# A ring of image rows in column-mod-4 order, read by patches with a stride of three

## The chip, the cores and the metric

The kernel runs on one core of one Trainium2 chip. The metric is the device time of one execution in microseconds (us); the median of several executions counts. A profile of one further execution is there for reading: it records every instruction of TensorE (PE, with its weight loads PEld), VectorE (DVE), ScalarE (ACT), GpSimd (POOL) and SyncE (SP), and the DMA traffic.

## The reference

Two blocks follow each other on `x` (4 images, 96 channels, 128×128, fp32). The first is a state-space block with four scans; the change does not touch it. The second is an attention over convolution maps:

```
xr, x1, x2 = relu_split_norm(gn(x))
key = unfold(conv3x3(x1, aw1))     # patches of 3x3, not overlapping: 42 x 42 of them
qry = unfold(conv3x3(x2, aw2))     # 96 channels x 9 taps x 1764 patches
attn = softmax(einsum("bckl,bqkl->bqck", key, qry) / sqrt(96 * 9))
value = conv3x3(x1, aw3)
y1 = layer_norm(conv3x3(value, attn as 3x3 weights))
y2 = layer_norm(conv3x3(x2, w_conv2)) * x1
out = x + xr + conv1x1(concat(y1, y2), w_full) + b_full
```

For every tap k of the 3×3 patch, key and query are thus multiplied over all patches: 96×96 products that sum over the pixels with row ≡ kh and column ≡ kw modulo 3. An image is 128 pixels wide, and 42 patches take 126 of them: columns 126 and 127, and rows 126 and 127, are in no patch.

## The kernel before

The program works through the four images. The first block of all images comes first. Image 0 then makes its maps (key, query, value, and `c2`, the convolution with `w_conv2`) in another way (`direct_maps`, with the class `Taps`), while the first block still runs. Images 1, 2 and 3 go through `attention`: a part that makes the maps, then a short part that turns the products into weights (`weights`: softmax, transposes), then a part that applies them to the value (`own` as the output tile). The norm and split of the next image and the output of the previous one run beside it ("light" work); generators are run in turn by `co_run`, which emits the instructions of the two in a ratio of costs. The last 20 or so microseconds of each map part, where the weights are made, are a chain with little beside it.

Convolutions in `attention` run in a column-tiled form (F(4,3), Winograd's): a row of 128 pixels is 32 tiles of four columns. Six planes per map are multiplied on TensorE and summed in PSUM pairs (`two`, three buffers of two banks). `outputs` takes them out: ScalarE copies two of the three pairs to SBUF (`ends`, `odd`, L1522), VectorE builds sums and differences (L1536–L1542), and four instructions at L1544, one for each column j of the tile, write the result:

```
for k, j, f in ((1, 1, AA), (2, 0, AA * AA), (0, 0, 1.0), (3, 1, AA**3)):
    if k == 0:
        nc.vector.tensor_add(v, ends, v)
    for p, e, o in parts:
        nc.vector.scalar_tensor_tensor(
            at(o, k), rows(w[p:e, j]), f, rows(v[p:e, j]), ALU.mult, ALU.add
        )
```

`at(o, k)` says where column k of all tiles lies in the output. Outputs that are kept in column-mod-4 order (first all 32 pixels with column ≡ 0 mod 4, then those ≡ 1, and so on: `own` and `oc` of images 1 to 3) get 32 adjacent words per row; outputs in plain order get every fourth word.

The maps are made in strips of 12 rows (eleven strips, the last of 8). For each strip and for m = 0 (inputs `x1p`: key and value) and m = 1 (`x2p`: query and `c2`), a first product of 128 output channels gives 96 channels of key or query and 32 of value or `c2`; a second gives the other 64. The first one's result goes to the ring: `rings[m]` of class `PairTaps`, room for two strips of 12 rows, plain order, rows of 129 words of which the last is zero. Rows lie in the order of their residue mod 3. `first_out` then copies the 32 value or `c2` channels (partitions 96 to 127) from the ring to `own` in column-mod-4 order, with three POOL copies, one for each residue of the row (L1967), and takes the statistics of the `c2` ones on VectorE (L1962).

`both` turns a pair of ring rows: for every tap it transposes 85 columns of the flat ring, three words apart, on TensorE (L1727). With two rows of 129 words, 43 columns come from the first row and 42 from the second. At this stride a row of 129 has 43 columns instead of 42, so the last one of the first row is in no patch; ScalarE multiplies it with zero while copying the PSUM pair to `kt`, with a scale for each partition (`patches`, L1732). `multiplied` (L1617) multiplies key and query patches, 85 rows to contract, and VectorE adds the result to `sm` (L1628, L1630).

The transposes of a strip are put in a list when both maps of that strip are written (`complete`), and are taken from the list between the products of the next strip (`some`). The order of the instructions on an engine is in these parts not the order of the code, but one made by the planner of the framework when the program is built.

`c2_weights` reads the statistics of `c2` (`c2a`) and sums them up.

Of the kernel before, what the change touches and what calls it, by code (L numbers as in the profile page):

```python
# [9 lines left out]
F32 = mybir.dt.float32  # L10
# [7 lines left out]
C = 96  # L18
# [11 lines left out]
PW = W + 1  # L30
# [2 lines left out]
TN = W // TW  # L33
PB = TN + 1
PP = PB * TW
AA = 2.0
AR = 12
LR = 8
# [31 lines left out]
def kernel(  # L70
# [1434 lines left out]
    def outputs(pool, m, n, parts, later, then):  # L1505

        got = []  # L1510

        def at(v, k):
            if len(v.shape) == 4:
                return v[:, :, k]
            return v.rearrange("p h (t k) -> p h t k", k=TW)[:, :, :, k]

        def rows(v):
            return v.rearrange("p (h t) -> p h t", t=TN)

        def copy_of(x, name, bufs):  # L1520
            t = pool.tile([128, 2, AR * TN], F32, name=name, bufs=bufs)[:m, :, :n]
            nc.scalar.copy(t, x[:m, :, :n])  # L1522
            return t

        def outer(c):
            later(lambda: got.append(copy_of(c, "ends", 2)))

        def sums(a, b):
            def first():
                t = copy_of(a, "odd", 1)  # L1530
                later(lambda: combined(t))

            def combined(t):
                w = pool.tile([128, 2, AR * TN], F32, name="wide", bufs=1)[:m, :, :n]
                ends, v = got[0], b[:m, :, :n]
                nc.vector.tensor_sub(w[:, 1], t[:, 1], v[:, 1])  # L1536
                nc.vector.tensor_add(w[:, 0], t[:, 1], v[:, 1])
                nc.vector.tensor_sub(v[:, 1], t[:, 0], v[:, 0])  # L1538
                nc.vector.tensor_add(v[:, 0], t[:, 0], v[:, 0])  # L1539
# [7 lines that stand above are left out]
                later(then)  # L1547

            later(first)

        return outer, sums
# [141 lines left out]
    class PairTaps(Taps):  # L1693
# [3 lines left out]
        def __init__(self, ps, later, pool):  # L1697
            self.ps, self.later, self.pool = ps, later, pool
            self.taps = [(0, 5), (5, KK)]
            self.sm = pool.tile([C, KK, C], F32, name="sm")  # L1700
            self.rings = [
                pool.tile([128, 2, AR, PW], F32, name=f"ring{i}", tag=f"ring{i}") for i in range(2)
            ]
            for t in self.rings:
                nc.gpsimd.memset(t[:, :, :, W:PW], 0.0)
            self.todo, self.rest = [], ()

        def flat(self, m):
            return self.rings[m].rearrange("p s r w -> p (s r w)")

        def part(self, m, n):
            return pairs_of(self.ps)[:m, 0, :n]

        def both(self, s, g, ks, kept):


            k0, k1 = ks
            n = (k1 - k0) * C
            pk = pairs_of(self.ps)[: 2 * NV + 1, :, :n]
            t = self.pool.tile([2 * NV + 1, 2, 5 * C], F32, name="kt", tag="kt", bufs=2)  # L1720
            slots = min(AR, H - s * AR + 1) // 3
            for m in (0, 1):
                kept[m] = t[:, m].rearrange("p (t o) -> p t o", o=C)
                for k in range(k0, k1):
                    kh, kw = divmod(k, 3)
                    o = (s % 2 * AR + kh * slots + 2 * g) * PW + kw
                    nc.tensor.transpose(  # L1727
                        pk[:, m, (k - k0) * C : (k - k0 + 1) * C],
                        self.flat(m)[0:C, o : o + 6 * NV + 1 : 3],
                        ident,  # L1730
                    )
            self.later(lambda: nc.scalar.activation(  # L1732
                t[:, :, :n], pk, AF.Copy, scale=patches[0 : 2 * NV + 1]
            ))
            self.later.tick()
            yield 0.3 * (k1 - k0)

# [180 lines left out]
    def attention(img, at):  # L1918
# [8 lines left out]
        if not img.mapped:  # L1927
# [21 lines left out]
            for s, (r0, r) in enumerate(chunks):  # L1949
                hr = r // 2  # L1950
                for m in (0, 1):
                    t, fill, load = at.strip()
                    r3 = (r + 2) // 3 * 3
                    to = taps.rings[m][:, s % 2, :r3]

                    def first_out(m=m, r0=r0, r=r, r3=r3, to=to):
                        v = to[96:128, :, 0:W].rearrange("p (q i) (t j) -> p q i j t", q=3, j=TW)
                        if m:
                            x = to[96:128, :, 0:W]
                            for q in range(0, r, 4):  # L1960
                                k = min(4, r - q)
                                nc.vector.bn_stats(img.c2a[96:128, 3 * (r0 // AR) + q // 4], x[:, q : q + k])  # L1962
                            d = last.rearrange("p (h j t) -> p h j t", j=TW, t=TN)
                        else:
                            d = vv[96:128]
                        for q in range(3):
                            nc.gpsimd.tensor_copy(d[:, q:r3:3], v[:, q])  # L1967
                        if m:
                            nc.sync.dma_start(
                                img.c2d[64:96, r0 * W : (r0 + r) * W], last[:, : r * W]  # L1970
                            )

                    evac = outputs(
                        p2, 128, r3 * TN, [(0, 128, to[:, :, 0:W])], later, first_out
                    )
                    yield from products(
                        ps, [(0, 128, 0, t, 0, r3)], pairs[m], later, evac, True,
                        [
                            both(fill[0], load[0]), fill[1], None, load[1]
                        ],  # L1980
                    )
                    yield from taps.some(1 if m else 2)
                    jobs = [(64 * q, 64 * q + 64, 128, t, q * hr, hr) for q in range(2)]
                    if m:
                        oc = pm.tile([128, AR // 2 * W], F32, name="oc", bufs=1)
                        to = [(0, 128, oc[:, : hr * W].rearrange("p (h j t) -> p h j t", j=TW, t=TN))]

                        def then(oc=oc, s=s, r0=r0, hr=hr):
                            per = 3 if hr % 4 else 4
                            for i in range(hr // per):  # L1990
                                nc.vector.bn_stats(
                                    img.c2b[:, 2 * s + i], oc[:, i * per * W : (i + 1) * per * W]
                                )
                            for q in range(2):
                                at = (r0 + q * hr) * W
                                nc.sync.dma_start(
                                    img.c2d[0:64, at : at + hr * W],
                                    oc[64 * q : 64 * q + 64, : hr * W],
                                )
                    else:  # L2000
                        to = [
                            (64 * q, 64 * q + 64, vv[0:64, q * hr : (q + 1) * hr])
                            for q in range(2)
                        ]
                        then = value_out(r0, r)
                    evac = outputs(p2, 128, hr * TN, to, later, then)
                    rest = products(ps, jobs, pairs[m], later, evac, fill=[
                        None, None, both(fill[2], load[2]), *fill[3:]
                    ])
                    if m and r0 + r == H:  # L2010
                        taps.rest = rest
                    else:
                        yield from rest
                        yield from taps.some(1 if m else 2)
                taps.complete(s, min(r, 3 * NV - r0))
# [133 lines left out]
    def c2_weights(img, ps, pool):  # L2149
# [2 lines left out]
        n = NSTRIP  # L2152
        mva, mvb = (pool.tile([128, 2], F32, name=f"mv_{i}") for i in "ab")
        for mv, st, p, e, k in (
            (mva, img.c2a, 96, 128, 4 * n - 1 if img.mapped else 3 * n - 1),
            (mvb, img.c2b, 0, 64, 2 * n - (not img.mapped)),
            (mvb, img.c2b, 64, 128, 2 * n - 1),
        ):
            v = st[p:e, :k].rearrange("p c s -> p (c s)")
            nc.vector.bn_aggr(mv[p:e], v)  # L2160
# [461 lines left out]
```

## Time and profile before

| what | value |
|---|---|
| median of 3 runs | 6576.74 us (6551.26 to 6590.82) |
| the profiled execution | 6563.7 us, of it span 6561.8 us |
| PE busy | 5379.6 us (82%) |
| DVE busy | 4887.7 us (74%) |
| ACT busy | 3826.6 us (58%) |
| POOL busy | 3510.5 us (53%) |
| mean granted clock of TensorE | 0.883 |
| maps of image 1, 2, 3 (span of L1727's stretches) | 3832–4530, 4718–5518, 5740–6332 us |

Busy times are unions over an engine's own instructions, so they say nothing alone on which engine sets the time. A row of the groups gives line, engine, operation, tiles, shape and count, then busy time and mean duration in nanoseconds, then the idle time of the engine right before them and what ended it. "two" is a PSUM pair, "ring", "kt", "own", "oc", "sm" are the tiles named above; "L1544" is a line of the kernel.

### The profile page before, as it was taken

To read this page: it belongs to the slowest core of one execution; us is meant where nothing else is said; L and a number is where in the kernel's file an instruction comes from. 1 tells how busy PE (TensorE), PEld (TensorE's weight loads), DVE (VectorE), ACT (ScalarE), POOL (GpSimd) and SP (SyncE) were. 2 spreads that over 40 slices of the span, in tenths; PEclk is the share of its full clock that TensorE was granted. 3 is DMA by queue.
4 is the path that set the end of the run, shared out by engine and by line. 5 is a ranking of instruction groups with operands and counts; after the bars stand their busy time and mean duration, and the time that the engine had idled before them with its cause. 6 is when DMAs were issued, how large, how long until landed. Compare 5 with 4: busy or idle time off the path is not lost. (4 is left out here: it accounts for less than half of the span.)

```text
span 6561.8 us, 75955 instructions
## 1 busy us (share of the span) xinstructions
PE 5379.6 (82%) x23264; PEld 2347.1 (36%) x23264; DVE 4887.7 (74%) x7229; ACT 3826.6 (58%) x4800; POOL 3510.5 (53%) x2649
## 2 busy tenths in 40 slices
PE   6889988987887735999897688877879777888888
PEld 2333323322222112444333243444324444344553
DVE  3247778988998778889745885587765788887866
ACT  1247767777787676777534554565444664544542
POOL 2236758978888546979521454465134574043420
PEclk9999989998998667999998788987988887998899
DMA  7767777775766757665676766655776555865658
GB/s 165 173 156 187 194 207 193 218 206 158 222 182 170 216 161 229 200 202 173 197 194 182 211 168 172 161 148 156 204 191 164 141 158 153 226 169 150 179 150 216
DMA packets 865058, 1198.50 MB, mean 183 GB/s; under 512 B 215598, under 2 KB 716054, under 8 KB 852172
## 3 DMA queue, kind: packets, MB, share of 16 engines
q1 hardware_dynamic: 841036, 1138.70, 63.7%
q0 software_dynamic: 16208, 38.42, 2.2%
q10 hardware_dynamic: 7408, 16.53, 0.8%
q8 instruction: 187, 3.06, 0.2%
q14 instruction: 219, 1.79, 0.1%
HBM read 777.82 MB, written 345.62 MB: 171 GB/s over the span
## 5 line engine op out<-in xcount | busy, mean ns | idle before, releaser
L622 PE MATMUL bank<-y,wp 128*128 128x512 f32 (+3 forms) x3584 | 1314.4, 624 | 85.9 <-DMA y<-y 34.6
L855 POOL TENSOR_TENSOR y<-y,dl 128x1024 f32<-128x1024 f32 x384 | 1059.3, 2759 | 267.8 <-DVE dl L847 245.7
L822 POOL TENSOR_TENSOR dl<-dl,u 128x1024 f32<-128x1024 f32 x384 | 1010.1, 2630 | 253.7 <-ACT dA L798 122.7
L843 DVE TENSOR_TENSOR_SCAN dA<-dA,pBC 128x512 f32<-128x512 f32 x768 | 981.5, 1278 | 30.7
L1451 PE MATMUL two<-ya,wd 128*64 128x192 f32 (+3 forms) x2376 | 597.2, 430 | 212.1 <-ACT odd L1522 102.4
L736 PE MATMUL pBC<-xr,wbc 60*128 60x512 bf16 (+1 forms) x1536 | 461.7, 405 | 326.3 <-DVE dA L843 253.5
L622 PEld LDWEIGHTS bank<-y,wp 128*128 128x128 f32 (+3 forms) x3584 | 457.3, 169 | 752.5 <-issue 655.0
L847 DVE TENSOR_TENSOR dl<-dA,pBC 128x512 f32<-128x512 f32 x768 | 528.0, 688 | 264.0 <-PE pBC L736 191.2
L2094 PE MATMUL bank<-y,wn 128*64 128x384 f32 (+5 forms) x2408 | 673.0, 504 | 54.5 <-DMA y<-x1d 31.6
L1897 ACT COPY yb<-ya 64x768 f32<-64x768 f32 (+1 forms) x660 | 537.9, 815 | 209.8 <-PE two L1451 138.8
L665 ACT ACTIVATE dl<-pd,dtb 128x512 f32<-128x512 f32 x768 | 485.6, 684 | 191.0 <-PE pd L736 167.3
L1451 PE MATMUL two<-yb,wd 128*64 128x192 f32 (+3 forms) x2376 | 569.8, 412 | 1.9 <-ACT yb L1897 1.9
L826 DVE TENSOR_TENSOR pBC<-dl,pBC 128x512 f32<-128x512 f32 x768 | 527.6, 687 | 8.3 <-POOL dl L822 7.3
L2094 PEld LDWEIGHTS bank<-y,wn 128*64 128x64 f32 (+3 forms) x2408 | 308.2, 168 | 345.9 <-issue 166.8
L798 ACT ACTIVATE dA<-dl,negA 128x1024 f32<-128x1024 f32 x384 | 420.3, 1141 | 2.3
L1451 PEld LDWEIGHTS two<-ya,wd 128*64 128x64 f32 (+1 forms) x2376 | 267.7, 172 | 424.4 <-ACT odd L1522 110.3
L736 PEld LDWEIGHTS <-wbc 60*128 60x128 bf16 (+1 forms) x1536 | 104.0, 96 | 769.4 <-issue 756.5
L665 ACT ACT_TABLE_LOAD x248 | 318.2, 1283 | 93.2 <-PE pd L736 80.2
L1967 POOL COPY own<-ring 32x512 f32<-32x512 f32 (+1 forms) x198 | 226.6, 1179 | 257.0 <-DVE ring L1544 220.6
L2203 POOL MEMSET o<- 1x1024 f32 x60 | 56.3, 946 | 571.3 <-PE bank L2258 256.7
L1451 PEld LDWEIGHTS two<-yb,wd 128*64 128x64 f32 (+1 forms) x2376 | 296.4, 173 | 153.6 <-issue 44.8
L1002 PE MATMUL bank<-y,outws 96*96 96x512 f32 x512 | 317.8, 759 | 9.5 <-DVE r L1015 6.3
(316 smaller groups left out, 9849.5 us busy)
## 6 DMA issues: line engine op xcount, KB each, us to landing
u<-zb SPq DMA_DIRECT2D x192, 1024.0 KB
yms<-y SPq DMA_DIRECT2D x96, 512.0 KB
y<-yms SPq DMA_DIRECT2D x64, 768.0 KB
xn<-xnew SPq DMA_DIRECT2D x128, 384.0 KB
ya<-vp SPq DMA_DIRECT2D x120, 336.0 KB
y<-y SPq DMA_DIRECT2D x128, 258.2 KB
zb<-z SPq DMA_DIRECT2D x64, 512.0 KB
ya<-x1p SPq DMA_DIRECT2D x90, 336.0 KB
```

The costliest lines, as they stand in the source:

```text
L622: nc.tensor.matmul(blocks(pz[p:e]), lhsT=ws[k][:, d, c : c + e - p], rhs=window(ys[k], at, d, n), start=(i == 0), stop=(i == len(terms) - 1),)
L665: nc.scalar.activation(dst, src, AF.Softplus, bias=bias)
L736: nc.tensor.matmul(p, lhsT=w[rows], rhs=xr[rows, at : at + CH], start=True, stop=True)
L798: nc.scalar.activation(live[m]["dA"], live[m]["dl"], AF.Exp, scale=negA[:, g % 3, k : k + 1])
L822: nc.gpsimd.tensor_mul(t, t, u_view(n))
L826: nc.vector.tensor_mul(p, live[n]["dl"][:, bass.ts(half, CH)], p)
L843: nc.vector.tensor_tensor_scan(h, h, p, init, ALU.mult, ALU.add)
L847: nc.vector.tensor_mul(live[n]["dl"][:, sl], live[n]["dA"][:, sl], live[n]["C", half])
L855: nc.gpsimd.tensor_add(v, v, t.rearrange("p (a b) -> p a b", b=W))
L1451: nc.tensor.matmul(of(to[p:e], r), lhsT=w[:, i, c : c + e - p], rhs=tiles(t[k][PAIR[i]][:, SLOT[i]], o, r), start=(k == 0), stop=False,)
L1897: nc.scalar.copy(yb[k][64 * h - 64 : 64 * h, :, :n], ya[k][0:64, :, h * TN : h * TN + n])
L2094: nc.tensor.matmul(pc[p:e, :n].rearrange("p (h w) -> p h w", w=W), lhsT=w[:, c : c + e - p], rhs=v[:, :, 0:W], start=(i == 0), stop=(i == ...
```

## The change

The ring takes the column-mod-4 order. A row is four blocks of 34 words (the last of 33), 135 in all: pixel 4t + j lies at word 34 j + t. Since 34 and 4 both leave 1 when divided by 3, the word's residue mod 3 is that of the pixel's column, and 135 is a multiple of three: a stride of three through two rows meets the 90 words of one residue, pixels of one kw and pads. The pads are set to zero when a `PairTaps` is made, and pixels 126 and 127 of the key are set to zero by two POOL memsets per strip (`cut`), so that nothing outside the patches is added. The scale in ScalarE's copy goes. The POOL copies are four (one for each column of the tile, 384 elements, the source packed) instead of three (512 elements, the source with a stride of four); the statistics of the 32 `c2` channels are four instructions of 384 elements instead of three of 512.

```diff
+JB = TN + 2
+JW = 3 * JB + TN + 1
@@ outputs
         def at(v, k):
+            if isinstance(v, list):
+                return v[k]
@@ PairTaps
-                pool.tile([128, 2, AR, PW], F32, name=f"ring{i}", tag=f"ring{i}") for i in range(2)
+                pool.tile([128, 2, AR, JW], F32, name=f"ring{i}", tag=f"ring{i}") for i in range(2)
             ]
             for t in self.rings:
-                nc.gpsimd.memset(t[:, :, :, W:PW], 0.0)
+                for j in range(TW):
+                    nc.gpsimd.memset(t[:, :, :, JB * j + TN : min(JB * (j + 1), JW)], 0.0)
...
+        def rows(self, m, s, r):
+            v = self.rings[m][:, s % 2, :r]
+            return [v[:, :, JB * j : JB * j + TN] for j in range(TW)]
+
+        def cut(self, s, r):
+            for j in (2, 3):
+                at = JB * j + TN - 1
+                nc.gpsimd.memset(self.rings[0][0:C, s % 2, :r, at : at + 1], 0.0)
@@ both
-            pk = pairs_of(self.ps)[: 2 * NV + 1, :, :n]
-            t = self.pool.tile([2 * NV + 1, 2, 5 * C], F32, name="kt", tag="kt", bufs=2)
+            cols = 2 * JW // 3
+            pk = pairs_of(self.ps)[:cols, :, :n]
+            t = self.pool.tile([cols, 2, 5 * C], F32, name="kt", tag="kt", bufs=2)
...
-                    o = (s % 2 * AR + kh * slots + 2 * g) * PW + kw
+                    o = (s % 2 * AR + kh * slots + 2 * g) * JW + kw
                     nc.tensor.transpose(
                         pk[:, m, (k - k0) * C : (k - k0 + 1) * C],
-                        self.flat(m)[0:C, o : o + 6 * NV + 1 : 3],
+                        self.flat(m)[0:C, o : o + 3 * cols - 2 : 3],
                         ident,
                     )
-            self.later(lambda: nc.scalar.activation(
-                t[:, :, :n], pk, AF.Copy, scale=patches[0 : 2 * NV + 1]
-            ))
+            self.later(lambda: nc.scalar.copy(t[:, :, :n], pk))
@@ attention
-                    to = taps.rings[m][:, s % 2, :r3]
+                    to = taps.rows(m, s, r3)
-                    def first_out(m=m, r0=r0, r=r, r3=r3, to=to):
-                        v = to[96:128, :, 0:W].rearrange("p (q i) (t j) -> p q i j t", q=3, j=TW)
+                    def first_out(m=m, s=s, r0=r0, r=r, r3=r3, to=to):
                         if m:
-                            x = to[96:128, :, 0:W]
-                            for q in range(0, r, 4):
-                                k = min(4, r - q)
-                                nc.vector.bn_stats(img.c2a[96:128, 3 * (r0 // AR) + q // 4], x[:, q : q + k])
+                            for j, v in enumerate(to):
+                                nc.vector.bn_stats(
+                                    img.c2a[96:128, TW * (r0 // AR) + j], v[96:128, :r]
+                                )
                             d = last.rearrange("p (h j t) -> p h j t", j=TW, t=TN)
                         else:
+                            taps.cut(s, r3)
                             d = vv[96:128]
-                        for q in range(3):
-                            nc.gpsimd.tensor_copy(d[:, q:r3:3], v[:, q])
+                        d = d[:, :r3].rearrange("p (i q) j t -> p q i j t", q=3)
+                        for j, v in enumerate(to):
+                            nc.gpsimd.tensor_copy(
+                                d[:, :, :, j], v[96:128].rearrange("p (q i) t -> p q i t", q=3)
+                            )
...
-                        p2, 128, r3 * TN, [(0, 128, to[:, :, 0:W])], later, first_out
+                        p2, 128, r3 * TN, [(0, 128, to)], later, first_out
@@ c2_weights
-            (mva, img.c2a, 96, 128, 4 * n - 1 if img.mapped else 3 * n - 1),
+            (mva, img.c2a, 96, 128, 4 * n - img.mapped),
```

## The prediction

> **What bounds the kernel now.** The change touches code that runs only while the maps of images 1, 2 and 3 are made, so I first looked for these stretches: the line that transposes the ring (L1727) runs in 3832–4530, 4718–5518 and 5740–6332 us. The view by stretches gives the busy time of each engine there (columns: stretch, its length, then busy time and number of instructions of PE, PE's weight loads, DVE, ACT and POOL, the granted clock, DMA):
>
> ```profile
> core 0: us, PE busy (x) PEld busy (x) DVE busy (x) ACT busy (x) POOL busy (x), PEclk, DMA share, GB/s
> 3832.00:4530.00 698.00, 568.19 (x3450) 319.01 (x3452) 481.51 (x913) 385.41 (x536) 393.45 (x499) 0.87 0.59 155
> 4718.00:5518.00 800.00, 649.53 (x3547) 346.89 (x3545) 587.64 (x1008) 422.35 (x570) 419.30 (x523) 0.85 0.59 160
> 5740.00:6332.00 592.00, 516.17 (x3226) 307.12 (x3226) 462.45 (x688) 298.33 (x368) 253.86 (x304) 0.92 0.60 162
> ```
>
> Together 2090 us, a third of the span. TensorE is busy for 1734 us (83%), VectorE for 1532 us (73%), so neither is full: the stretch is TensorE's work and its waits, 356 us idle. The view of waits, TensorE alone, 3832–6332 us, tells on whom it waits (total, times, longest):
>
> ```profile
> PE two L1451 <- ACT odd L1522: 107.7, 37, 10.6
> PE two L1451 <- ACT ends L1522: 43.5, 20, 5.4
> PE two L1451 <- ACT kt L1732: 35.0, 21, 7.1
> PE two L1451 <- DVE sm L1630: 20.3, 15, 4.3
> PE two L1617 <- DVE ring L1544: 17.2, 9, 3.2
> PE two L1617 <- ACT odd L1522: 15.0, 12, 2.9
> PE two L1451 <- DVE ring L1544: 7.6, 9, 2.8
> ```
>
> These are waits for a PSUM pair to come free: ScalarE's copies (L1522, L1732) and VectorE's ring writes (L1544) free them. The same view for the other two engines shows a second way from the ring to TensorE, by way of POOL and ScalarE:
>
> ```profile
> POOL own L1967 <- DVE ring L1544: 220.6, 30, 24.2
> ACT x L1403 <- POOL pl L1416: 103.9, 43, 7.5
> ```
>
> POOL stands at the head of its queue until the ring is written; ScalarE, in order, waits for POOL's later work, and its evacuations (L1522) are behind that.
>
> The rows of the groups that the change touches (mean ns after the bar), then line 1544 writing `own` in 3692–3832 us, where rows are plain (stride of four), and in 4552–4717 us, where they are in blocks of 32:
>
> ```profile
> L1544 DVE SCALAR_TENSOR_TENSOR ring<-wide,two 128x384 f32<-128x384 f32 x240 | 189.8, 868 | 2.6
> L1967 POOL COPY own<-ring 32x512 f32<-32x512 f32 x180 | 210.0, 1202 | 231.4 <-DVE ring L1544 196.4 <-issue 32.9 <-POOL pl L1381 0.6
> L1967 POOL COPY own<-ring 32x384 f32<-32x384 f32 x18 | 16.6, 954 | 25.6 <-DVE ring L1544 24.2 <-issue 1.3
> L1962 DVE BATCH_NORM_STATS2 c2a<-ring 32x6 f32<-32x512 f32 x96 | 61.1, 680 | 1.3
> L1732 ACT ACTIVATE kt<-two,patches 85x960 f32<-85x960 f32 x63 | 65.4, 1050 | 29.8 <-PE two L1727 28.3
> L1727 PE MATMUL two<-ident,ring 96*85 96x96 f32 x1134 | 162.0, 293 | 23.0 <-ACT odd L1522 14.3 <-DVE d L194 5.2 <-DVE sm L1630 1.5
> L1544 DVE SCALAR_TENSOR_TENSOR own<-wide,two 96x384 f32<-96x384 f32 x40 | 31.2, 860 | 3.4 <-DMA od<-own 3.0
> L1544 DVE SCALAR_TENSOR_TENSOR own<-wide,two 96x384 f32<-96x384 f32 x40 | 20.2, 553 | 0.9 <-DMA od<-own 0.5
> ```
>
> The last two rows are the experiment already made: the same instruction, one size, 860 ns with a stride of four and 553 ns in blocks.
>
> [...] a row of 135 begins every second row at an odd word. [...] the value's rows, pitch 33, have odd blocks too and took 349 ns for 192 columns, `oc` with even blocks 345. [...] The strided copies here cost (1202 − 954) / 128 = 1.94 ns an element and 0.21 us fixed; no run yet shows the packed one.
>
> **The change part by part.** There are 3 images with 11 strips, key (m = 0) and query (m = 1) in each.
>
> Ring writes. 240 of 384 columns go from 868 to 553 ns: −75.6 us. 24 of 288 columns, interpolated from the rows of 256 (609 strided; 410 in blocks, the fastest of `o`) and 384: 672 to 446 ns, −5.4. VectorE −81 us, and the last write of each ring half ends 4 × 0.315 = 1.26 us earlier.
>
> Statistics. 96 instructions of 512 (680 ns, 65.3 us) become 132 of 384 or 256 (556 and 423 ns at L1761, which reads the other ring): 120 × 556 + 12 × 423 = 71.8 us, +6.5. If runs of 32 cost the full 680 ns each, +24. VectorE net −74 us, within −57 and −76. The twelve more entries in the aggregate of c2_weights (32 to 44) are three instructions of well under 1 us.
>
> Copies of the last 32 channels on POOL. 3 of 512 become 4 of 384. With the strided price 4 × 954 = 3.82 us against 3 × 1202 = 3.61: +0.21, +14 us over 66 sets. [...] The 66 new memsets of pixels 126 and 127 (`cut`) are priced by L1705 (128×24 in 144 ns): +9.5 us. Six memsets of pads become 24, at the starts of images: +3. POOL −40 us likely, +27 at worst.
>
> The patches' copy to `kt`: the per-partition scale goes. Plain copies are 792 ns for 768 columns and 0.83 ns a column more (L1897: 829 − 670 over 192), so 951 for 960: −99 ns, 126 of them, ScalarE −12.5 us. [...]
>
> Transposes and products: 90 columns for 85. L1601 does the same with 128 columns: weights 205 ns against 208 here, matmul 286 against 293; L1617 there contracts 128 rows in 266 ns, here 85 in 275. So nothing, and at most 5 columns by 1 ns by 1134 = 6 us if a weight load does grow. No DMA is added, moved or resized: SP's `c2d` store waits for a fourth POOL copy instead of a third.
>
> The new wait. Transposes of a key strip now need POOL's `cut`, not only VectorE. In 6140–6320 us:
>
> ```profile
> 6269.28 3.14 POOL L1967 COPY own<-ring 32x512 f32<-32x512 f32 x3 [7.03 <-DVE ring L1544]
> 6299.75 2.59 PE L1727 MATMUL two<-ident,ring 96*85 96x96 f32 x20
> ```
>
> The copies stand where `cut` will, and the first transposes of that strip come 30 us later (some 18 in the last strip). I cost the wait at nothing under that cover; behind it on TensorE would be every product of the next strip.
>
> What of it reaches the end. (a) TensorE waits 26.3 us in 20 waits for ring writes (17.2, 7.6 and 1.5 at L1727), 1.3 us each; 1.26 can go from each, I take three quarters: 20. (b) It waits 28 us in 19 waits for `sm` (L1630, L1628), queued behind ring writes; with a third just behind: 6 × 1.26 = 8. (c) 26 waits for `kt`, 0.1 each: 3. (d) 80 waits, 181 us, for L1522; if one in eight is held by POOL, which is now 1.26 earlier and each set 0.8 shorter: 10 × 1.3 = 13. (e) Between last strip and weights TensorE idles; 0.9 less in three places: 3. Sum 47 us. Where a wait goes, the next one (ScalarE's own queue, or the light work's POOL and DMA waits) ends it, for which I take off a fifth: **38 us**. On the profiled execution (span 6561.8, time 6563.7) that is 6526; it is 13 us under the median of 6576.7, so against the median 6539.
>
> **Rivals.** *Covered* (0.14): TensorE's work sets the pace and the freed VectorE time is idle time. For it: 83% busy, 0.92 clock in the third stretch. Against: 26 us of direct waits. 10 us, 6567. *VectorE sets the pace* (0.10): all of 74 + 12.5 is saved, 6490. For it: VectorE leads wherever TensorE stands; against: most of the waits name ScalarE. *Blocks do not stream* (within the first case's range): [...] *Slower by the cut* (0.21): engines here do not run in the order of the code (L1628 stands between L1537 and L1538 at 4942 us), and the order is made anew. POOL waits up to 24.2 us at its head. If `cut` comes over 30 us after the ring, TensorE's transposes stop, and 3 us of excess by 33 strips is +99, less 38: 6638. From 2.2 us of excess a strip it is over 0.5% slower. Against: the largest lag that I saw in a steady strip was 14 us. A worse order without this mechanism belongs here too.
>
> **How the numbers follow.** My own case has 0.55, with gains of 20 to 60 us; 0.38 of that lies above 33 us, which is 0.5%, about what a measurement of this kernel can tell from no change. With 0.10 of the second rival, faster is 0.48. Same: 0.17 + 0.14 + 0.03 = 0.34. Slower 0.18. The runs before spread over 40 us. Range: the larger gain and a little (6480), and part of the slower case (6600).
>
> **What would show it.** L1544 on `ring` near 553 ns; `kt` copies near 950 and 790; POOL's copies near 0.70 us; VectorE busy 74 us less; PE's waits for L1544 near 6 us; no TensorE wait that names the memset. I am wrong if `ring` writes stay above 0.7 us, if TensorE's idle time in the three stretches stays near 356 us, or if the memset appears among its releasers.

## The result and the profile after

The changed kernel took 6516.18 us (median of 6 runs, 6508.89 to 6531.86) beside 6577.02 us of the kernel before (6 runs): a ratio of 0.9908 with a 95% interval of 0.9889 to 0.9927, 61 us less. A second measurement (e4 below) gave 0.9919 (0.9901 to 0.9937), 53 us. Where one figure is needed I take 0.9913, which lies between the two, and 57 us. The profiled execution took 6520.1 us, its span 6518.3.

First the groups of the profile after that answer to the rows shown of before (line, engine, operation, tiles, shape, count, then busy us and mean ns, then the idle time before them and what ended it). The ring write is now L1548, POOL's copy L1983, the statistics L1974, ScalarE's copy L1749, the transposes L1744:

```profile
L1548 DVE SCALAR_TENSOR_TENSOR ring<-wide,two 128x384 f32<-128x384 f32 x240 | 122.3, 548 | 2.7
L1983 POOL COPY own<-ring 32x384 f32<-32x384 f32 x240 | 125.7, 544 | 182.9 <-DVE ring L1548 163.3 <-issue 13.0 <-POOL pl L1383 1.1
L1974 DVE BATCH_NORM_STATS2 c2a<-ring 32x6 f32<-32x384 f32 x120 | 63.6, 551 | 2.7
L1749 ACT COPY kt<-two 90x960 f32<-90x960 f32 x63 | 58.8, 950 | 29.2 <-PE two L1744 27.7
L1744 PE MATMUL two<-ident,ring 96*90 96x96 f32 x1134 | 131.9, 265 | 31.2 <-ACT odd L1526 20.7 <-DVE ring L1548 7.2 <-DVE sm L1634 2.2
```

Four of these are what was forecast or better: ring writes 868 to 548 ns, statistics 551, `kt` 1050 to 950, and POOL's packed copies 544, where my estimate, which no run had shown, was 700. The fifth was not foreseen at all: the transposes' busy time fell from 162.0 to 131.9 us, though each now moves 90 columns instead of 85.

Then the view by stretches, for the three times in which the maps are made (length, busy time and count of PE, PE's weight loads, DVE, ACT, POOL, granted clock, DMA):

```profile
3841.00:4517.00 676.00, 546.74 (x3446) 304.35 (x3444) 460.36 (x925) 381.06 (x536) 368.76 (x543) 0.88 0.60 160
4700.00:5485.00 785.00, 623.13 (x3552) 326.69 (x3553) 567.20 (x1025) 417.36 (x569) 390.00 (x563) 0.87 0.60 163
5705.00:6287.00 582.00, 505.60 (x3228) 294.48 (x3228) 433.02 (x702) 294.25 (x368) 224.17 (x348) 0.92 0.60 166
```

The stretches shrank from 2090 to 2043 us, 47 us: the gain lies in the parts that the change touches. In them VectorE is busy 71 us less (1531.6 to 1460.6) and POOL 84 us less (1066.6 to 982.9). TensorE's idle time, however, did not shrink: 2043 less 1675.5 is 368 us, before 356. Its busy time fell by 58 us, of which the transposes are 30; what a busy time from a single profile can tell is taken up at e9.

Last the waits of TensorE in 3841–6287 us (total, times, longest); the lines that I had counted on:

```profile
PE two L1453 <- ACT odd L1526: 121.3, 36, 10.1
...
PE two L1621 <- DVE ring L1548: 14.4, 8, 4.4
...
PE two L1453 <- DVE ring L1548: 8.6, 7, 3.2
...
PE two L1744 <- DVE ring L1548: 7.2, 2, 5.7
```

The waits for ring writes are 30.2 us in 17 waits; they were 26.3 in 20. From this trace alone one would say that the faster ring writes missed their target, and that the shorter transposes made the gain. The experiments speak against both readings.

### The profile page after: what moved, and what is told of

Read it like the earlier page. It is cut to its first block, busy times and chain, and to the rows that moved or that the text cites. A ratio compares the mean times of both kernels' runs of the same rounds, so it can differ in the third digit from the quotient of the medians.

```text
span 6518.3 us, 76253 instructions
## 1 busy us (share of the span) xinstructions
PE 5323.7 (82%) x23264; PEld 2300.7 (35%) x23264; DVE 4813.2 (74%) x7265; ACT 3816.2 (59%) x4800; POOL 3426.6 (53%) x2799
## 5 line engine op out<-in xcount | busy, mean ns | idle before, releaser
L2112 PE MATMUL bank<-y,wn 128*64 128x384 f32 (+5 forms) x2408 | 673.8, 505 | 53.2 <-DMA y<-x1d 28.1
L1383 POOL TENSOR_TENSOR pl<-x 128x192 f32<-128x192 f32 (+2 forms) x456 | 307.8, 690 | 0.2
```

Source lines behind the costliest of these rows:

```text
L2112: nc.tensor.matmul(pc[p:e, :n].rearrange("p (h w) -> p h w", w=W), lhsT=w[:, c : c + e - p], rhs=v[:, :, 0:W], start=(i == 0), stop=(i == ...
```

## The experiments

Each was timed in 5 rounds beside the kernel before on the same chip; ratios are to that. Three chips: e1 to e4 (before: 6572.29 us), e5 to e8 (6556.10), e9 to e12 (6558.42). The planner makes the order anew for each program, so the orders of the engines were compared, by line and output tile in the traces: for e1, e2, e5 and e9 they are those of the kernel before, for e3 that of the kernel after. Between before and after they differ: at some 260 of the 23264 places in TensorE's order and 136 of the 4800 in ScalarE's another instruction stands.

**e1: only the number of columns.** The kernel before, with 86 transposed columns instead of 85.

```diff
-            pk = pairs_of(self.ps)[: 2 * NV + 1, :, :n]
+            pk = pairs_of(self.ps)[: 2 * NV + 2, :, :n]
-                        self.flat(m)[0:C, o : o + 6 * NV + 1 : 3],
+                        self.flat(m)[0:C, o : o + 6 * NV + 4 : 3],
```

> The kernel before with one more column in the transposes of the ring, 86 instead of 85 (the 86th is the next row's column that the mask already sets to zero); nothing else is changed, and every engine's order of instructions is that of before. Theory 1 (the saved TensorE time comes from the number of columns: 85 is odd, 90 is even): the weight loads of L1727 fall from 204 to about 155 ns and the transposes' busy time from 162 to about 130 us; as TensorE sets the pace of these stretches, the whole is 25 to 35 us faster (ratio 0.995 to 0.996). Rival (the shorter loads come from the new layout or from the missing mask): the loads stay at 204 ns, ratio 1.000.

Measured: 6574.16 us, ratio 1.000 (0.9988 to 1.0012). The weight loads of the transposes, before and then e1 (lowest, median and highest ns, then first to last), show that the operation did change:

```profile
L1727 PEld LDWEIGHTS two<-ident,ring x1134: 192/204/268, 3877.9 to 6328.5; 96*85 96x85 f32 x189
```

```profile
L1727 PEld LDWEIGHTS two<-ident,ring x1134: 152/155/197, 3887.7 to 6340.4; 96*86 96x86 f32 x189
```

And the stretch from the first map of image 1 to the last of image 3, first before, then e1:

```profile
3661.00:6352.00 2691.00, 2217.09 (x11835) 1180.47 (x11835) 2018.78 (x3403) 1442.18 (x1893) 1197.32 (x1490) 0.87 0.64 171
```

```profile
3666.00:6364.00 2698.00, 2188.42 (x11835) 1144.99 (x11835) 2022.22 (x3405) 1441.91 (x1893) 1198.18 (x1490) 0.87 0.63 171
```

TensorE works 29 us less and the stretch is not shorter. All of it came back as waits: summed over the view of waits in this stretch, TensorE's waits for ScalarE rose from 255.8 to 278.6 us and those for VectorE from 173.7 to 185.7. So this work of TensorE does not set the length of the stretch, though TensorE is busy for 2217 of its 2691 us. The even count gave nothing that an interval of 8 us to each side lets see.

**e2: only VectorE's writes.** The kernel before, with L1544 writing the ring in four blocks of 32, rows unchanged.

```diff
         def at(v, k):
+            if isinstance(v, list):
+                return v[k]
-                        p2, 128, r3 * TN, [(0, 128, to[:, :, 0:W])], later, first_out
+                        p2, 128, r3 * TN, [(0, 128, [to[:, :, TN * k : TN * (k + 1)] for k in range(TW)])], later, first_out
```

> The kernel before in which line 1544 writes the ring in four blocks of 32 adjacent words per row (rows stay 129 long, 85 columns, three copies, mask kept); the pixels then stand in the wrong order, so key, query and the last 32 channels of value and c2 are of permuted columns. It is the saving of VectorE alone: 81 us of its busy time. The prediction's sum (34 us for ring releases, the sums behind them and what POOL starts earlier): ratio about 0.995. Rival (TensorE sets the pace and VectorE's time was covered): within 10 us, ratio 0.9985 or more.

Measured: 6537.22 us, 0.9945 (0.9927 to 0.9963), 36 us. Here, in an unchanged order, the waits for ring writes are (TensorE, 3660–6313 us):

```profile
PE two L1619 <- DVE ring L1546: 11.8, 6, 3.2
...
PE two L1729 <- DVE ring L1546: 5.4, 2, 4.6
...
PE two L1451 <- DVE ring L1546: 2.0, 2, 1.7
```

That is 19.2 us where before had 26.3: they did fall, by 7 us, and all waits of TensorE for VectorE in the stretch fell from 173.7 to 147.1 us. The stretch itself:

```profile
3660.00:6313.00 2653.00, 2200.34 (x11834) 1176.48 (x11835) 1949.80 (x3404) 1442.70 (x1893) 1193.02 (x1490) 0.88 0.64 173
```

It is 38 us shorter: 21 us are idle time of TensorE and 17 us busy time (see e9). Why the waits for ring writes do not fall in the kernel after, no run separates; its order is another one.

**e3: the kernel after with an odd count**, 89 columns; one column of patches is left out of the products.

```diff
-            cols = 2 * JW // 3
+            cols = 2 * JW // 3 - 1
```

> The kernel after with 89 instead of 90 columns in the transposes of the ring: one patch column of each second row is left out of the sums; nothing else is changed, and the order on every engine is that of after. Theory 1 (odd number of columns): weight loads go from 159 back to about 204 ns, and the time is 25 to 35 us over that of the kernel after (ratio to before about 0.995 to 0.996). Rival (layout or mask): loads stay at 159 ns and the time is that of after.

**e4: the kernel after once more**, on this chip.

> The kernel after once more, on the chip of the other three, as their measure: ratio 0.989 to 0.993.

Measured: e3 6522.16 us, 0.9925 (0.9908 to 0.9942); e4 6518.27 us, 0.9919 (0.9901 to 0.9937). The transposes of e3 are back at the long form:

```profile
L1744 PE MATMUL two<-ident,ring 96*89 96x96 f32 x1134 | 169.8, 300 | 28.4 <-ACT odd L1526 19.0 <-DVE ring L1548 6.7 <-DVE sm L1634 2.0
```

38 us more of TensorE's time than in the profile after, and 4 us in the end beside e4, well inside the intervals (about 11 us to each side). The same answer from the other side as e1.

**e5: VectorE's writes and POOL's copies.** e2, with POOL's three copies of 512 elements reading runs of 32.

```diff
-                        v = to[96:128, :, 0:W].rearrange("p (q i) (t j) -> p q i j t", q=3, j=TW)
+                        v = to[96:128, :, 0:W].rearrange("p (q i) (j t) -> p q i j t", q=3, j=TW)
```

> The kernel of e2 (ring written in blocks of 32 into rows of 129; key and query of permuted columns) in which POOL's three copies per set also read the ring in blocks, packed, 512 elements each; the order on every engine is still that of before. Theory 2 (VectorE's ring writes give about 36 us, POOL's cheaper copies a part of the remaining 20, since ScalarE and with it the release of PSUM pairs waits for POOL): 10 to 20 us below e2, ratio 0.9915 to 0.993. Rival (POOL is hidden; the rest is ScalarE's or a better order): the same as e2, 0.9945. The copies should take about 0.65 to 0.7 us.

Measured: 6499.36 us, 0.9909 (0.9894 to 0.9925), 60 us. The copies took 662 ns for 512 elements where the kernel before needs 1202:

```profile
L1969 POOL COPY own<-ring 32x512 f32<-32x512 f32 x180 | 112.9, 662 | 211.0 <-DVE ring L1546 183.3 <-issue 25.3 <-POOL pl L1381 0.7
```

With the order, the columns, the scale and the statistics of the kernel before, these two edits alone gain as much as the whole change.

**e6: the kernel after with POOL's copies strided again**, three of 512; the values that it copies stand in another order.

```diff
-                        for j, v in enumerate(to):
-                            nc.gpsimd.tensor_copy(d[:, :, :, j], v[96:128]...)
+                        v = taps.rings[m][96:128, s % 2, :r3, 0:W].rearrange("p (q i) (t j) -> p q i j t", q=3, j=TW)
+                        for q in range(3):
+                            nc.gpsimd.tensor_copy(d[:, q:r3:3], v[:, q])
```

> The kernel after with POOL's copies as before: three of 512 that read every fourth word of the ring's rows (the value and c2 of the last 32 channels are then of the wrong pixels); TensorE and VectorE have the order of after. POOL has about 85 us more to do. Theory 2: 10 to 20 us slower than after (ratio to before about 0.994). Rival (POOL hidden): as after, 0.991 to 0.992.

Measured: 6545.07 us, 0.9978 (0.9968 to 0.9987). TensorE, VectorE and ScalarE keep the order of after. Of the 57 us, some 43 are lost when POOL alone is slow: (0.9978 − 0.9913) × 6556, with some 10 us of doubt to each side.

**e7: the kernel after with the scale operand kept** in ScalarE's copies.

```diff
-            self.later(lambda: nc.scalar.copy(t[:, :, :n], pk))
+            self.later(lambda: nc.scalar.activation(t[:, :, :n], pk, AF.Copy, scale=patches[0:cols]))
```

> The kernel after with the copies to kt again multiplied with a scale for each partition (the old mask: two of 90 patch columns are set to zero, so a few patches are left out): ScalarE has 126 x 0.1 = 12.5 us more to do. Theory 2: TensorE waits for these copies 26 times in the stretches, so 3 us, at most 12 us slower than after (0.992 to 0.9935). Rival (ScalarE is what sets the pace once VectorE is shorter): over 12 us slower.

Measured: 6526.16 us, 0.9953 (0.9940 to 0.9965), some 26 us slower than after by the ratios. Between before and after, a copy without the operand is 100 ns shorter for 960 columns (1050 to 950) and 102 for 768 (891 to 789), which makes 12.7 us of ScalarE's time for the 126 copies; 26 is more than that, and at some 290 places of TensorE's order and 144 of ScalarE's stands another instruction than in the kernel after. Read it with e11.

**e8: the kernel after with fewer instructions for POOL and VectorE.** Three copies of 512 elements instead of four of 384, statistics of four whole rows (512) in fewer instructions, and one memset for both columns of `cut`.

```diff
+        def some_rows(self, m, s, q, k):
+            v = self.rings[m][96:128, s % 2, q : q + k, 0:TN]
+            p, row, one = v.ap
+            return bass.AP(v.tensor, v.offset, [p, row, [JB, TW], one])
...
-            for j in (2, 3):
-                at = JB * j + TN - 1
-                nc.gpsimd.memset(self.rings[0][0:C, s % 2, :r, at : at + 1], 0.0)
+            at = 2 * JB + TN - 1
+            nc.gpsimd.memset(self.rings[0][0:C, s % 2, :r, at : at + JB + 1 : JB], 0.0)
...
-                        for j, v in enumerate(to):
-                            nc.gpsimd.tensor_copy(d[:, :, :, j], v[96:128]...)
+                        for q in range(3):
+                            nc.gpsimd.tensor_copy(d[:, q:r3:3], taps.some_rows(m, s, q * (r3 // 3), r3 // 3))
```

> The kernel after with three POOL copies of 512 (packed) instead of four of 384, three statistics of 512 instead of four of 384, and one memset of two words a row instead of two for pixels 126 and 127: same results. VectorE has 7 us less, POOL about 25 us less. Theory 2: 3 to 10 us faster than after (ratio 0.990 to 0.9915). Rival (a different order of the plan decides): anything within 15 us of after, also slower.

Measured: 6477.62 us, 0.9881 (0.9864 to 0.9898): the best version, 78 us under the kernel before and by the ratios some 21 under the kernel after. Its copies:

```profile
L1988 POOL COPY own<-ring 32x512 f32<-32x512 f32 x180 | 112.4, 659 | 34.7 <-issue 27.2 <-DVE ring L1548 4.4
```

The shape says where the four copies of the change lose: 4 × 544 = 2.18 us a set against 3 × 659 = 1.98. POOL's idle time right before the copies is 34.7 us instead of 182.9 only because in this order the memset of `cut` stands ahead of them and takes the wait for the ring (203.5 us). Its order is not that of after either (some 230 places differ for TensorE, 186 for ScalarE). Which of its three edits brought how much of the 21 us, and how much the order, I did not separate.

**e9: only POOL's copies.** The line of e5's diff alone, on the kernel before.

> The kernel before in which only POOL's three copies read the ring packed (words side by side instead of every fourth, so the last 32 channels of value and c2 have permuted columns); ring writes, mask and 85 columns stay, and the order on every engine is that of before. POOL has about 95 us less to do. If POOL's copies count by themselves (e5 was 24 us under e2, e6 40 us over after): 20 to 40 us faster, ratio 0.994 to 0.997. Rival (they count only once VectorE's writes are shorter, since POOL stands waiting for these): within 8 us, 0.999 or more.

Measured: 6522.05 us, 0.9945 (0.9932 to 0.9958), 36 us. VectorE's writes are the slow ones of before, so this is POOL alone. Its group and its stretch:

```profile
L1967 POOL COPY own<-ring 32x512 f32<-32x512 f32 x180 | 117.5, 687 | 251.3 <-DVE ring L1544 202.2 <-issue 31.6 <-DMA ya<-x1p 15.5
```

```profile
3654.00:6312.00 2658.00, 2194.51 (x11835) 1173.74 (x11835) 2002.92 (x3405) 1442.94 (x1893) 1101.56 (x1490) 0.88 0.63 173
```

The stretch is 33 us shorter, with 96 us less of POOL's time. Who had waited for POOL is seen in the waits of VectorE and ScalarE, first before (VectorE, 3661–6352 us), then e9 (VectorE, then ScalarE, 3654–6312):

```profile
DVE xstats L1029 <- POOL r L1023: 82.1, 46, 5.9
...
DVE half L1247 <- POOL pl L1413: 45.9, 15, 7.2
```

```profile
DVE xstats L1029 <- POOL r L1023: 75.9, 44, 5.9
...
DVE half L1247 <- POOL pl L1413: 37.1, 12, 7.3
```

```profile
ACT x L1403 <- POOL pl L1416: 97.7, 41, 7.5
```

VectorE waits 15 us less for POOL, in the norm and split of the next image and the output of the last one; ScalarE's wait fell from 103.9 to 97.7, and all its waits for POOL from 211.2 to 198.3. VectorE's own queue holds the ring writes and the sums into `sm`, so what POOL gives back there can reach TensorE. By the same sum over the view of waits, TensorE's waits for VectorE fell from 173.7 to 163.3 us and those for ScalarE not at all (255.8, 256.2). That accounts for 10 of the 33 us. The other 23 are busy time of the same 11835 matmuls, up to 3% less each in most groups and up to 1% more in others. One pair of profiles can't say that this part is the copies' doing: e5 and e10 have the same order on TensorE, and their profiles differ by 17 us in its busy time (5371.1 and 5354.2 over the program) and by 1 us in the time of the execution.

The granted clock moves along with it, 0.886 in this profile and 0.883 in that of before, and here a rival stays open. In the 134 timed executions with a clock on record (those of the experiments, of the kernel before beside them, and of the kernel after), 0.001 more of clock than the mean of the same kernel on the same chip goes with about 2.7 us less of time. The executions of e9 have a mean clock of 0.8862 and those of before beside them 0.8826, which by this slope would be some 10 of its 36 us; for e2 it is 6, for e8 some 14. The mean clock is higher than before's by 0.0019 or more in all experiments but e1, e6 and e7, which are the three with the smallest gains. Whether it is higher because of the edits, no run here separates.

**e10: the new wait and its memsets.** e5, with two memsets of `cut` on POOL ahead of each key strip's copies (columns 95 and 127 of the ring, both of the last residue in that layout).

```diff
+                            for c in (95, 127):
+                                nc.gpsimd.memset(taps.rings[0][0:C, s % 2, :r3, c : c + 1], 0.0)
                             d = vv[96:128]
```

> The kernel of e5 (blocks and packed copies in the order of before; columns permuted) with two memsets of a column of the key's ring for each strip put ahead of POOL's copies, as `cut` does: 66 memsets of 0.12 us; TensorE, VectorE and ScalarE keep their order. My step (the wait of the transposes is covered by 18 to 30 us): within 8 us of e5, 0.991 to 0.992. Rival (POOL's start is on the path, or transposes wait for it): 15 us and more, 0.993 or more.

Measured: 6502.59 us, 0.9911 (0.9898 to 0.9923), beside e5's 0.9909; TensorE, VectorE and ScalarE run in e5's order. The memsets, and what each costs (lowest, median, highest ns):

```profile
L1968 POOL MEMSET ring<- x66: 108/116/139, 3839.9 to 6250.6; 96x12 f32 x60, 96x9 f32 x6
```

The wait and its 66 memsets of 116 ns cost nothing that this measurement can tell.

**e11: no scale.** e5, with the plain copy to `kt`; the column that the scale set to zero is then added to the products.

```diff
-            self.later(lambda: nc.scalar.activation(t[:, :, :n], pk, AF.Copy, scale=patches[0 : 2 * NV + 1]))
+            self.later(lambda: nc.scalar.copy(t[:, :, :n], pk))
```

> The kernel of e5 with the plain copy to kt (no mask, so one false patch column of the 85 is summed): ScalarE has 12.5 us less; the plan moves 55 of TensorE's rows. ScalarE counts (e7 was 26 us over after): 10 to 25 us under e5, 0.987 to 0.9895. My step (c), 3 us: 0.990 to 0.991. A different order could also make it slower.

Measured: 6496.57 us, 0.9901 (0.9885 to 0.9918), 5 us under e5 by the ratios and inside the intervals; by the traces, some 110 places of TensorE's order and 103 of ScalarE's differ from e5's.

**e12: the kernel after without `cut`**; pixels 126 and 127 of the key are then added to the products.

```diff
-                            taps.cut(s, r3)
```

> The kernel after without `cut` (pixels 126 and 127 of the key are not set to zero, so one false patch column is summed): 8 us of POOL's time less, but the plan puts TensorE's and VectorE's work in another order in many places. Together with e10 it shows what a changed order alone does: within 8 us of after (0.990 to 0.993) if order matters little, 15 us or more to either side if it does.

Measured: 6507.15 us, 0.9919 (0.9906 to 0.9933): no gain over after, as in e10. The expectation counted on another order of TensorE's and VectorE's work. The traces do not show one: by line, tiles and shape, TensorE, VectorE and ScalarE run in the order of the kernel after. So e12 is a second test of the wait, and says nothing on what an order weighs.

## Why the prediction was right, and where it was not

The forecast of 6539 us (38 us of gain) lies on the right side and holds the measured time in its range; the gain of 53 to 61 us is about half as large again. That the sum came so near is in part luck: the direct waits in (a) gave a good third of what it put there, POOL in (d) gave about three times as much. By its steps:

- **Ring writes** (81 us of VectorE): right, 548 ns for a forecast of 553. (For 288 columns I interpolated 672 ns; the profile of before has a row for them, 690.) Net of the statistics VectorE's busy time fell by 74.5 us over the whole program (4887.7 to 4813.2) against 74. What of it reaches the end, steps (a), (b) and (e), was 31 us, or 25 after the deduction of a fifth; e2 shows 36. The size was fair; the place was not. I had (a) take 20 of 26.3 us from TensorE's direct waits for L1544, leaving about 6. In e2 only 7 us went there, and in the kernel after the sum rose to 30.2. Of the 27 us less waiting for VectorE, (b) brought nothing: the waits for `sm` (L1628, L1630) went from 28.1 to 30.9 us. The other 20 us are mostly waits for norms (L1015, L2160, L192, L194). The 17 us that TensorE is busy less stay open as in e9.
- **POOL's copies**: this is the term that was mis-sized. The price failed first: 544 ns measured, 700 estimated. The 700, and with it the 0.8 us a set in (d) and the 40 us of POOL, were my estimate and shown by no run. From 384 elements in 544 ns (after) and 512 in 659 (e8) the packed price is 0.90 ns an element, 0.46 of the strided 1.94. A set fell by 3 × 1202 − 4 × 544 = 1.43 us instead of 0.8. But step (d) failed more: I gave 13 us to ScalarE held by POOL, and e9 shows 36 alone, e5 over e2 some 24, e6 some 43 in the order of after. The sum was too small by its own figures (1.26 + 0.8 is 2.06 us a wait, not 1.3), but even with the whole of 1.26 + 1.43 us for each of its ten waits, (d) would have given 27. And its way is not the one that e9 shows: ScalarE waited 13 us less for POOL, yet TensorE's waits for ScalarE stayed the same. One way that the sum lacked is VectorE's own waits for POOL (82.1 and 45.9 us), in the light work whose rows I had not listed because the change does not touch them. They fell by 15 us, and TensorE's waits for VectorE by 10. How the rest of the 36 us reaches the end is not shown.
- **The deduction of a fifth** for waits that follow: not borne out in sum. Alone, the two edits give 36 and 36 us, together 60; that falls short of 72 by a sixth, but the intervals of about 8 to 12 us to each side do not exclude plain addition.
- **Transposes and products at nothing**: right for the time, by the wrong argument. I compared 85 columns with the 128 of L1601 and saw no effect of the count. There was one of 45 ns a load: between 85 and 90 columns it goes with odd and even (medians of 204 and 210 ns for 85 and 89, 155 and 159 for 86 and 90). It counts for nothing that e1 (29 us less of TensorE's work, ratio 1.000) and e3 (38 us more of the transposes' time, 4 us beside e4) could tell, because this time of TensorE is not the limit. The 1 ns a column in the forecast's bound was an estimate; L1451's weight loads in before took 155 ns for 64 columns and 205 to 207 for 128, 0.8 ns a column.
- **"The stretch is TensorE's work and its waits"**: as a statement of what sets the length, this failed. In e1 29 us less work became 35 us more waiting. What fits e1, e2 and e9 is that the way from TensorE's pair over the other engines back to a free pair sets the pace; VectorE and POOL are shown to count in it (36 us each, e2 and e9), ScalarE is not (e7 and e11 leave it open). With that, the test that I set was the wrong one: idle time of TensorE near 356 us was to mean that I am wrong, and it is 368 with a gain of 47 us in the stretches.
- **The new wait at nothing**: right. No wait of TensorE names the memset; e10 and e12 agree. The rival *slower by the cut* falls with it.
- **The scale** (12.5 us of ScalarE): its price was exact, 1050 to 950 ns for a forecast of 951. Its worth, 3 us in (c), stays open: e11 gives 5 us, e7 gives 26 for the reverse, each with another order of instructions.
- **The rivals.** *Covered* falls. *VectorE sets the pace* (6490) came closer in size than in cause: half of VectorE's 69 to 75 us reaches the end (e2). *Blocks do not stream* falls: the ring writes took 548 ns, though every second row begins at an odd word; the forecast was 553.

Not settled: the kernel after has everything that e5 has and more, and comes to the same 0.991; e6 has e2's writes and is about 22 us slower than e2. Both suggest that something in the new order or in the additional instructions takes some of the gain back. The even count (e1, e3) and the wait with its memsets (e10, e12) are not it as far as these runs can tell; the four copies can't be it in e6, which has three. That leaves the additional statistics on VectorE and the order. e8 gets 21 us more with fewer instructions of POOL and VectorE, but in yet another order, and its edits were not run one by one.

## What to carry to other kernels

A high busy share and long waits of one engine don't make it the one that sets the pace: shorten that engine's work alone (here by one column more, in the same order: 29 us less work, ratio 1.000) and see whether the time moves. When an edit frees an engine, look up all that wait for it, also in work that the edit does not touch; here POOL's copies, filed under side effects, were worth as much as the VectorE writes that the edit was about (36 us each, e9 and e2). A layout that turns one engine's strided writes into packed ones can pay a second time where another engine reads the same data (here VectorE's write went from 868 to 548 ns, POOL's copy of 512 elements from 1202 to 662 in e5), so count all who write and read a layout before choosing it.

## What the runs showed of the hardware

- In these four kernels, loading an fp32 matrix of an odd number of columns into TensorE took longer than one of an even number: medians 204 ns for 85 (before) and 210 for 89 (e3), 155 for 86 (e1) and 159 for 90 (after), all read at a stride of three words from the same kind of tile. The matmul behind it has a median of 281 and 287 ns, or 246. 128 columns, read at the same stride at L1601 of the kernel before, took a median of 210 ns.
- A POOL copy of 32 × 512 fp32 took 1202 ns with its source four words apart (before) and 659 to 687 in runs of 32 (e5, e8, e9).
- A VectorE write of 128 × 384 fp32 into the ring took 868 ns with its words four apart (before) and 546 to 548 in runs of 32 (e5, after), though every second row begins at an odd word.
- A one-column memset of 96 × 12 on POOL took a median of 116 ns (e10).
